# Preparing the first pair of graphs side by side, with early loads of the adjacency and late loads of the weights

## The chip, the cores and the metric

The kernel runs on one core of a Trainium2 chip. The metric is the device time of one execution in microseconds (us), of which the median over several runs is taken. The engines are named as in the profile: PE (TensorE), DVE (VectorE), ACT (ScalarE), POOL (GpSimd) and SP (SyncE, which only issues transfers here).

## The reference

There are 16 graphs of 1024 nodes with 64 channels, a symmetric 0/1 adjacency of 1024 x 1024 and a node mask. Two layers follow each other, each as `x = x + layer(relu(layernorm(x)))`. What matters here is the first one:

```python
neigh = (adj_ > 0) & ~eye
rank = jnp.cumsum(ni, axis=-1) - ni
skip = jnp.where(nb > T, (nb + K - 1) // K, 1)            # T, K = 10, 2
rem = neigh & (sk > 1) & (rank % sk == sk - 1) & mask[:, :, None]
rem = rem | jnp.swapaxes(rem, 1, 2)
adj_d = jnp.where(rem, 0.0, adj_)
vals = jnp.where(nd[..., None], x[:, None, :, :], jnp.inf)
s = jnp.sort(vals, axis=2)
...                                                       # quartiles of s, weighted, summed into agg
h = jax.nn.relu((x + agg) @ W1 + b1)
y = h @ W2 + b2
```

So some edges are dropped, symmetrically; then, for each node and channel, the values of the remaining neighbours are sorted, and their three quartiles make the aggregate. The second layer is three graph convolutions with the undropped adjacency, each with a batch norm, and a last linear layer over all three results.

## The kernel before, in words

The graphs are handled in eight pairs, the 64 channels of the two graphs of a pair lying side by side on the 128 partitions. For each pair there are three kinds of work.

`prepare` (L582) makes the pair ready: it normalizes the rows (`room`, L563), stores them (`h_d`, L598), and for each graph calls `prepare_one`. That loads the adjacency in eight tiles of 128 x 1024 fp32 (`a`, 512 KB, L664, two buffers), makes each into fp8 edges on ACT (L671), checks on DVE that it holds only 0 and 1 (`junk_v`, L673), transposes it on PE (L678) and evicts the transposed tile on ACT (`edgeT`, L681). `edgeT` is stored for the second layer (`adjT_d`, L684), and after that store DVE clears its diagonal in place (L686). Sums over chunks and prefix sums follow on PE (`tot` L646, `cs` L716 and L721), an absolute value on ACT and a comparison on DVE (`stays`, L725 and L726: which edges stay), the symmetric combination on PE (`q`, L736 to L747), and its eviction on ACT with the number of live neighbours (L752). Then nodes are ranked by that number (`keys` L763 on PE, eight signs `junk` L770 on ACT), and `place` (L773, DVE) says where each row goes. POOL scatters the rows to `live_d` (L778) and later fetches them back in that order (`lp`, L794, two buffers); PE transposes them again (L809), ACT evicts (`liveT`, L812), and PE and ACT number the slots of each row (`pr` L845, `r` L851), in two sides: the first 592 columns within `prepare`, the other 432 later through `st.number`.

`gather_block` takes a range of nodes: DVE makes selection matrices (`s`, L987), PE multiplies them with the rows (`pg`, L1018), and ACT copies the result (`g`, L1023). `sort_block` runs a sorting network on DVE over it (L935). There are seven such blocks to a pair, with the sort of one block woven with the gather of the next and with the preparation of the next pair, in parts given by `SHARES`.

The order on each engine comes from the framework's scheduler: it takes what is ready, and among that what was written first in the program. Tiles with one tag share a fixed number of buffers, and a new tile waits until the last reader of an old one is done. In PSUM the preparation has two buffers (`big`), used by the transposes, `tot`, `cs`, `q`, `keys`, `pt` and `pr` of both graphs. `stays`, `junk` and `junk_v` have one buffer; the four fp8 arrays `edge`, `edgeT` and `liveT` of a pair share four (`byte`).

Before all that come constants and the weights: 48 small transfers from ACT's queue (`weight`, `column`, `row`, `both`, L499 to L518) and a few operations on the batch norm's columns (L531 to L537). They are used only by the second layer and the linear parts of the first, in `first_layer` and `next_layer`, which run beside the last pair and after it.

Pair 0 is prepared alone, before the first gather:

```python
ahead = Steps(prepare(0, early))
ahead.rest()
```

Of the kernel before, what the change touches and what calls it, by code (L numbers as in the profile page):

```python
# [10 lines left out]
F32 = mybir.dt.float32  # L11
F16 = mybir.dt.float16
BF16 = mybir.dt.bfloat16
F8 = mybir.dt.float8e4
I32 = mybir.dt.int32
U8 = mybir.dt.uint8
AF = mybir.ActivationFunctionType
ALU = mybir.AluOpType
# [4 lines left out]
P = 128  # L23
C = 64
HID = 128
LN_EPS = 1e-5
BN_EPS = 0.001
# [2 lines left out]

SHARES = (10, 9, 17, 24, 20, 13, 0)
STEPS = 7

MAGIC = 8388608.0

# [362 lines left out]
            pass  # L398


@with_exitstack
def graph_layers_kernel(ctx: ExitStack, tc: tile.TileContext, ins, out: bass.AP):
    nc = tc.nc
    x_d, adj_d, mask_d = ins["x"], ins["adj"], ins["nodemask"]
    NB, N, _ = x_d.shape
    NT = N // P
# [86 lines left out]

    odd = const.tile([P, NB, NT], F32, name="odd")

    def weight(name, rows, cols, twice=False):
        t = const.tile([rows * (1 + twice), cols], F32, name=f"w_{name}")
        for k in range(1 + twice):
            nc.scalar.dma_start(out=t[k * rows : (k + 1) * rows, :], in_=ins[name])  # L499
        return t  # L500

    def column(name, rows, twice=False):
        t = const.tile([rows * (1 + twice), 1], F32, name=f"c_{name}")
        for k in range(1 + twice):
            nc.scalar.dma_start(out=t[k * rows : (k + 1) * rows, :], in_=ins[name].rearrange("(p o) -> p o", o=1))
        return t

    def row(name, cols):
        t = const.tile([P, cols], F32, name=f"r_{name}")
        nc.scalar.dma_start(out=t, in_=ins[name].partition_broadcast(P))  # L510
        return t

    def both(t, src):

        nc.vector.memset(t, 0.0)
        for k in range(2):
            half = slice(k * C, (k + 1) * C)
            nc.scalar.dma_start(out=t[half, half], in_=src)  # L518


    w1 = weight("L0_gnn_W1", C, HID, True)
    w2 = weight("L0_gnn_W2", HID, C)
    b1 = column("L0_gnn_b1", HID)
    b2 = row("L0_gnn_b2", C)
    layers = []
    for i in (1, 2, 3):
        wl = const.tile([P, P], F32, name=f"wl{i}")
        both(wl, ins[f"L1_gnn_W{i}"])
        bl, g, be, m, v = (column(f"L1_gnn_{k}{i}", C, True) for k in ("b", "g", "be", "m", "v"))
        s = const.tile([P, 1], F32, name=f"bn_s{i}")  # L530
        nc.vector.tensor_scalar(s, v, BN_EPS, None, ALU.add)  # L531
        nc.scalar.activation(s, s, AF.Sqrt)
        nc.vector.reciprocal(s, s)
        nc.vector.tensor_tensor(s, s, g, ALU.mult)

        nc.vector.tensor_tensor(m, m, s, ALU.mult)
        nc.vector.tensor_tensor(be, be, m, ALU.subtract)  # L537
        layers.append((wl, bl, s, be))
    wlast = const.tile([P, 3, P], F32, name="wlast")
    for i in range(3):  # L540
        both(wlast[:, i, :], ins["L1_gnn_Wl"][i * C : (i + 1) * C, :])
    blast = row("L1_gnn_bl", C)

    biases = {}

    def bias(value):

        if value not in biases:
            t = const.tile([P, 1], F32, name=f"bias{len(biases)}")
            nc.vector.memset(t, value)  # L550
            biases[value] = t
        return biases[value]

    def rows_of(ap):
        return ap.rearrange("(t p) c -> p t c", p=P)
# [26 lines left out]
        pass  # L582


    def prepare(p, pools):


        work, keep, ps = pools
# [3 lines left out]
        xt, h, sq = room[:, 0], room[:, 1], room[:, 2].rearrange("p x t c -> p (x t) c")  # L592
        for x in range(2):
            nc.sync.dma_start(out=xt[:, x], in_=rows_of(x_d[2 * p + x]))
        flat = "p x t c -> p (x t) c"
        layernorm_relu(work, h.rearrange(flat), xt.rearrange(flat), sq, T2)
        for x in range(2):
            nc.sync.dma_start(out=rows_of(h_d[2 * p + x][:, :]), in_=h[:, x])  # L598
        yield
        st.g = {}  # L600
        st.nvs = keep.tile([P, N], BF16, tag="nvs", bufs=2, name="nvs")
        r0 = keep.tile([P, 2, NT, SPLIT], BF16, tag="r0", name="r0")
        r1 = keep.tile([P, 2, NT, N - SPLIT], BF16, tag="r1", name="r1")
        st.r = (r0, r1)
        find_live, number_slots = [], []
        for x in range(2):
            find_live.append((yield from prepare_one(st, x, pools)))
        for x in range(2):
            number_slots.append((yield from find_live[x]()))
            yield from number_slots[x](0)  # L610


        st.z = keep.tile([P, len(TAUS), N], BF16, tag="z", name="z")
# [15 lines left out]
        yield  # L629
        st.number = itertools.chain(*(number_slots[x](1) for x in range(2)))  # L630
        return st

    def diagonal(e):

# [19 lines left out]
    def prepare_one(st, x, pools):  # L654
# [5 lines left out]
        edge = work.tile([P, NT, N], F8, tag="byte", bufs=4, name="edge")  # L660
        edgeT = work.tile([P, NT, N], F8, tag="byte", bufs=4, name="edgeT")
        def load(t):
            a = work.tile([P, N], F32, tag="a", bufs=2, name="a")
            nc.sync.dma_start(out=a, in_=adj_d[b, t * P : (t + 1) * P, :])  # L664
            return a
# [3 lines left out]
        for t in range(NT):  # L669
            a, coming = coming, load(t + 1) if t + 1 < NT else None  # L670
            nc.scalar.activation(edge[:, t, :], a, AF.Sign, saturate=False)  # L671
            junk = work.tile([P, N], F8, tag="junk_v", name="junk_v")
            nc.vector.scalar_tensor_tensor(  # L673
                junk, a, 1.0, a, ALU.is_equal, ALU.not_equal, accum_out=odd[:, b, t : t + 1], saturate=False
            )
            pt = ps.tile([P, NT, P], F32, tag="big", bufs=2, name="ptE")
            for u in range(NT):
                nc.tensor.matmul(  # L678
                    out=pt[:, u, :], lhsT=edge[:, t, u * P : (u + 1) * P], rhs=ident_h, start=True, stop=True
                )  # L680
            nc.scalar.activation(edgeT[:, :, t * P : (t + 1) * P], pt, AF.Copy, saturate=False)  # L681
            yield

        nc.sync.dma_start(out=adjT_d[b][:, :, :], in_=edgeT)  # L684
# [46 lines left out]
        for t in range(NT):  # L731
            q = ps.tile([P, N], F32, tag="big", bufs=2, name="q")
            for hf in range(NH):
# [15 lines left out]
                        start=False, stop=(u % 4 == 3),  # L749
                    )  # L750

            nc.scalar.activation(  # L752
                edge[:, t, :], q, AF.Relu, bias=bias(-2.0), accum_out=nv[:, t : t + 1], saturate=False
            )
            yield

        key = work.tile([P, NT], F32, tag="key", name="key")
# [30 lines left out]
        def find_live():  # L788
# [16 lines left out]
            for t in range(NT):  # L805
                lp, coming = coming, fetch(t + 1) if t + 1 < NT else None
                pt = ps.tile([P, NT, P], F32, tag="big", bufs=2, name="pt")
                for u in range(NT):
                    nc.tensor.matmul(  # L809
                        out=pt[:, u, :], lhsT=lp[:, u * P : (u + 1) * P], rhs=ident_h, start=True, stop=True  # L810
                    )
                nc.scalar.activation(liveT[:, :, t * P : (t + 1) * P], pt, AF.Copy, saturate=False)  # L812
                yield

            half = slice(x * C, (x + 1) * C)
# [22 lines left out]
            def number_slots(side):  # L838

                j0, j1 = ((0, SPLIT), (SPLIT, N))[side]  # L840
                for u in range(NT):
                    pr = ps.tile([P, N], F32, tag="big", bufs=2, name="pr")
                    for a in range(j0, j1, HALF):
                        sl, o = slice(a, min(a + HALF, j1)), slice(a - j0, min(a + HALF, j1) - j0)
                        nc.tensor.matmul(out=pr[:, o], lhsT=upto, rhs=liveT[:, u, sl], start=True, stop=(u == 0))  # L845
                        if u:
# [1 line left out]
                                out=pr[:, o], lhsT=before[:, u : u + 1].to_broadcast([P, P]), rhs=sums[:, sl],  # L848
                                start=False, stop=True,
                            )  # L850
                    nc.scalar.copy(st.r[side][:, x, u, :], pr[:, : j1 - j0])  # L851
                    if u % 2:
                        yield

# [565 lines left out]
    with ExitStack() as stack:  # L1420
# [7 lines left out]
        with ExitStack() as inner:  # L1428
# [1 line left out]
                inner.enter_context(tc.tile_pool(name="early", bufs=1)), keep,  # L1430
                inner.enter_context(tc.tile_pool(name="ps_early", bufs=1, space=PSUM)),
            )
            ahead = Steps(prepare(0, early))
            ahead.rest()
            st = ahead.result
            first, *_ = gather_block(st, 0, pools)
# [1 line left out]
            for p in range(NP - 1):  # L1438
# [7 lines left out]
                for n in range(last):  # L1446
# [16 lines left out]
                    else:  # L1463
                        weave(sort_block(st, n, pools), gather_block(st, n + 1, pools), steps)
                st = to_come
            for _ in st.number:
                pass

# [69 lines left out]
```

## Time and profile before

| what | value |
|---|---|
| median of three runs | 3166.65 us (3160.47 to 3176.45) |
| the profiled execution | 3163.56 us, of which the span is 3161.8 us |
| busy in the span | PE 82%, DVE 81%, ACT 54%, POOL 20% |
| first edges on ACT (L671) | 32.53 us |
| `place` of graphs 0 and 1 (L773) | 109.09 and 161.33 us |
| first selection of the main phase (`s`, L987) | 205.80 us |
| start of the later pairs' `z` copies on POOL (L1065), pairs 1 and 2 | 511.42 and 811.48 us |

All positions are counted from the start of the span. In the answers quoted below, a timeline row gives the start, the length, the engine, the line and operation, what is written from what with its shape, how many instructions were merged, and in brackets how long the engine had been idle and what released it. A row of groups gives the count, the busy time and the mean of one in ns, and the idle time before.

### The profile page before, as it was taken

To read this page: it belongs to the slowest core of one execution; us is meant where nothing else is said; L and a number is where in the kernel's file an instruction comes from. 1 tells how busy PE (TensorE), PEld (TensorE's weight loads), DVE (VectorE), ACT (ScalarE), POOL (GpSimd) and SP (SyncE) were. 2 spreads that over 40 slices of the span, in tenths; PEclk is the share of its full clock that TensorE was granted. 3 is DMA by queue.
4 is the path that set the end of the run, shared out by engine and by line. 5 is a ranking of instruction groups with operands and counts; after the bars stand their busy time and mean duration, and the time that the engine had idled before them with its cause. 6 is when DMAs were issued, how large, how long until landed. Compare 5 with 4: busy or idle time off the path is not lost.

```text
span 3161.8 us, 67201 instructions
## 1 busy us (share of the span) xinstructions
PE 2599.2 (82%) x27849; PEld 1697.4 (54%) x27849; DVE 2559.8 (81%) x5895; ACT 1696.2 (54%) x3292; POOL 619.5 (20%) x545
## 2 busy tenths in 40 slices
PE   2678978898888889885798889888986688977778
PEld 1445655565556556653565566456643456644445
DVE  4149889998999799989998999899976979963332
ACT  4764666567557755774367557745853223332221
POOL 5110161022102200330022103300422530311110
PEclk9779999999899999997899999999987799988989
DMA  4131022111211212122111211211113011122211
GB/s 138 46 104 60 3 67 70 56 55 52 66 57 54 64 56 68 46 72 47 42 64 51 66 56 57 67 56 63 48 36 75 9 41 26 49 55 54 54 54 42
DMA packets 221082, 177.45 MB, mean 56 GB/s; under 512 B 189024, under 2 KB 189152, under 8 KB 216672
## 3 DMA queue, kind: packets, MB, share of 16 engines
q1 hardware_dynamic: 141824, 125.88, 13.1%
q0 software_dynamic: 17408, 37.81, 3.9%
q10 hardware_dynamic: 61536, 9.39, 1.7%
q8 instruction: 219, 3.59, 0.5%
q14 instruction: 95, 0.78, 0.1%
HBM read 124.44 MB, written 48.55 MB: 55 GB/s over the span
## 4 chain that ended last, share of the span: by engine, by line
DVE 40%; PE 29%; ACT 12%; DMA 8%; issue 6%; another core or an unknown queue 2%; POOL 2%; ACTq 1%; DVEq 0%; POOLq 0%; SPq 0%
PE pg L1018 11%; DVE t L935 10%; DVE s L987 9%; DVE g L935 8%; PE pg L1200 5%; ACT junk L770 3%; DMA a<-in_adj 3%; DMA lp<-live_d 3%; DVE junk_v L673 2%; PE pr L845 2%; DVE g_tails L935 1%; DVE t_tails L935 1%; PE keys L763 1%; PE pf L1216 1%
## 5 line engine op out<-in xcount | busy, mean ns | idle before, releaser
L1018 PE MATMUL pg<-s,hp 128*64 128x400 bf16 (+11 forms) x16848 | 1366.5, 313 | 172.3 <-DVE s L987 138.1
L1018 PEld LDWEIGHTS <-hp 128*64 128x64 bf16 x16848 | 894.5, 112 | 553.9 <-issue 109.6
L987 DVE TENSOR_SCALAR s<-r 128x3200 bf16<-128x3200 bf16 (+25 forms) x1312 | 623.6, 521 | 103.6 <-PE pg L1018 74.9
L778 POOL DMA_INDIRECT live_d<-edge,place x128 | 261.1, 2040 | 1354.3 <-DVE place L773 1149.9
L1023 ACT COPY g<-pg 128x400 f32<-128x400 f32 (+10 forms) x384 | 169.0, 443 | 399.4 <-PE pg L1018 363.1
L935 DVE TENSOR_TENSOR t<-g 128x600 f32<-128x600 f32 (+9 forms) x524 | 315.5, 626 | 34.0 <-ACT g L1023 33.2
L1200 PE MATMUL pg<-adjT,xw 128*64 128x512 fp8e4 x2304 | 284.5, 398 | 52.8 <-ACT xw L1185 25.7
L935 DVE TENSOR_TENSOR g<-t 128x96 f32<-128x96 f32 (+16 forms) x555 | 283.2, 537 | 1.2
L1243 POOL DMA_INDIRECT agg<-agg_d,place x128 | 171.2, 1338 | 495.2 <-PE pt L1131 258.2
L671 ACT ACTIVATE edge<-a 128x1024 fp8e4<-128x1024 f32 x128 | 135.1, 1058 | 214.4 <-DMA a<-in_adj 213.9
L1200 PEld LDWEIGHTS <-xw 128*64 128x64 bf16 x2304 | 140.1, 114 | 182.4 <-issue 42.0
L868 ACT ACTIVATE coef<-z,bias 128x200 f32<-128x200 bf16 (+6 forms) x480 | 173.9, 405 | 102.3 <-DVE agg L950 66.0
L935 DVE TENSOR_TENSOR t<-t 128x192 f32<-128x192 f32 (+20 forms) x447 | 207.8, 475 | 0.2
L871 ACT ACTIVATE coef<-coef,wcol 128x200 f32<-128x200 f32 (+7 forms) x512 | 189.6, 403 | 9.3 <-issue 7.1
L673 DVE SCALAR_TENSOR_TENSOR junk_v<-a 128x1024 fp8e4<-128x1024 f32 x128 | 155.4, 1214 | 24.4 <-DMA a<-in_adj 24.4
L845 PE MATMUL pr<-liveT,upto 128*128 128x512 fp8e4 (+2 forms) x384 | 127.4, 350 | 53.1 <-ACT r L851 46.9
L770 ACT ACTIVATE junk<-keys,minus 128x1024 fp8e4<-128x1024 f32 x128 | 144.3, 1128 | 38.1 <-PE keys L763 34.3
L851 ACT CAST r<-pr 128x592 bf16<-128x592 f32 (+1 forms) x256 | 142.5, 585 | 41.1 <-PE pr L847 32.1
L794 POOL DMA_DIRECT2D lp<-live_d x128 | 89.4, 699 | 376.9 <-PE pt L809 319.3
L812 ACT ACTIVATE liveT<-pt 128x1024 fp8e4<-128x1024 f32 x128 | 130.3, 1034 | 50.5 <-PE pt L809 47.1
L752 ACT ACTIVATE edge<-q,bias 128x1024 fp8e4<-128x1024 f32 x128 | 141.8, 1108 | 22.6 <-PE q L747 22.6
L725 ACT ACTIVATE stays<-cs,back 128x1024 f16<-128x1024 f32 x128 | 136.7, 1111 | 31.1 <-PE cs L721 15.9
(182 smaller groups left out, 3879.4 us busy)
## 6 DMA issues: line engine op xcount, KB each, us to landing
a<-in_adj SPq DMA_DIRECT2D x128, 512.0 KB
adjT_d<-edgeT SPq DMA_DIRECT2D x16, 1024.0 KB
lp<-live_d POOLq DMA_DIRECT2D x128, 128.0 KB
adjT<-adjT_d SPq DMA_DIRECT2D x16, 1024.0 KB
room<-in_x SPq DMA_DIRECT2D x16, 256.0 KB
h_d<-room SPq DMA_DIRECT2D x16, 256.0 KB
h_again<-h_d SPq DMA_DIRECT2D x16, 256.0 KB
xt<-in_x SPq DMA_DIRECT2D x16, 256.0 KB
```

The source lines that it names most:

```text
L673: nc.vector.scalar_tensor_tensor(junk, a, 1.0, a, ALU.is_equal, ALU.not_equal, accum_out=odd[:, b, t : t + 1], saturate=False)
L770: nc.scalar.activation(junk, keys, AF.Sign, bias=minus[:, t : t + 1], accum_out=above[:, t : t + 1], saturate=False)
L778: sent = nc.gpsimd.indirect_dma_start(out=live_d[b][:, :], out_offset=bass.IndirectOffsetOnAxis(ap=place[:, b, t : t + 1], axis=0), in_=ed ...
L845: nc.tensor.matmul(out=pr[:, o], lhsT=upto, rhs=liveT[:, u, sl], start=True, stop=(u == 0))
L868: nc.scalar.activation(coef[:, i, :], z[:, at], AF.Abs, bias=bias(rank - (slots + 1) // 2 + tau), scale=sign)
L871: nc.scalar.activation(coef[:, i, :], coef[:, i, :], AF.Relu, bias=wcol[:, q : q + 1], scale=-w)
L935: nc.vector.tensor_tensor(view(bufs, o, n1, n2), view(bufs, a, n1, n2), view(bufs, b, n1, n2), ALU.max if op else ALU.min)
L987: nc.vector.tensor_scalar(s[:, k, :, us, w0:], r[:, :, us, at + w0 : at + W], float(LIVE + 1 + k0 + k), None, ALU.is_equal)
L1018: summed = nc.tensor.matmul(out=pg[x * C : (x + 1) * C, ks, w0:], lhsT=st.hp[:, part, x, u, :], rhs=s[:, ks, x, u, w0:], start=(whole and ...
L1023: nc.scalar.copy(g[:, k0 : k0 + n, :], pg)
L1200: nc.tensor.matmul(out=pg[cs, :], lhsT=part[:, u, cs], rhs=adjT[x][:, u, sl], start=(u == 0 and k == 0), stop=(u == NT - 1 and k == len(xw ...
L1243: nc.gpsimd.indirect_dma_start(out=agg[:, t, x, :], out_offset=None, in_=agg_d[b][:, :], in_offset=bass.IndirectOffsetOnAxis(ap=place[:, b ...
```

## The change

For pair 0 alone, the adjacency is loaded in 16 transfers into `homes`: buffers of the tags `g`, `t`, `s` and `agg`, which the main phase uses later, and the two of `a`. The steps of the two graphs are written alternately (`side_by_side`), with graph 1 twelve steps behind. The checks (`check`) of pair 0 are written after all its other steps up to the slot numbers. Of its evictions `edgeT`, `liveT`, `r` and the counting one of `q`, every second (`t % 2`) goes to DVE. The weights' loads and the operations on them are written after the second round of the loop over pairs (`p == WEIGHTS`), from SP's queue, and wait for the last gather matmul of pair 2's first block (`behind`).

```diff
+WEIGHTS = 1
+def side_by_side(one, other):
+    while one.step():
+        other.step()
...
+    behind = None
+    def load_weight(t, src):
+        tc.add_manual_dep(
+            nc.sync.dma_start(out=t, in_=src).ins, behind.ins.name,
+            mybir.DependencyInfo(mybir.DependencyClass.Sync, mybir.DependencyReason.DATA),
+            reason="not among the first loads",
+        )
...
-            nc.scalar.dma_start(out=t[k * rows : (k + 1) * rows, :], in_=ins[name])
+            load_weight(t[k * rows : (k + 1) * rows, :], ins[name])
...
+        def check(b, t, a):
+            junk = work.tile([P, N], F8, tag="junk_v", name="junk_v")
+            nc.vector.scalar_tensor_tensor(
+                junk, a, 1.0, a, ALU.is_equal, ALU.not_equal, accum_out=odd[:, b, t : t + 1], saturate=False
+            )
...
+        for k, home in enumerate(homes):
+            nc.sync.dma_start(out=home, in_=adj_d[2 * p + k // NT, k % NT * P : (k % NT + 1) * P, :])
...
+        if homes:
+            one, other = (Steps(prepare_one(st, x, pools)) for x in range(2))
+            for _ in range(4 + NT):
+                one.step()
+            side_by_side(one, other)
+            find_live = Steps(one.result())
+            side_by_side(find_live, other)
+            other.rest()
+            number_slots.append(find_live.result)
+            find_live = Steps(other.result())
+            side_by_side(Steps(number_slots[0](0)), find_live)
+            find_live.rest()
+            number_slots.append(find_live.result)
+            yield from number_slots[1](0)
+            for k, home in enumerate(homes):
+                check(2 * p + k // NT, k % NT, home)
...
+    def evict(st, t, o, i):
+        if st.homes and t % 2:
+            nc.vector.tensor_scalar(o, i, 1.0, None, ALU.mult, saturate=o.dtype != F8)
+        else:
+            nc.scalar.activation(o, i, AF.Copy, saturate=o.dtype != F8)
...
-            nc.scalar.activation(edgeT[:, :, t * P : (t + 1) * P], pt, AF.Copy, saturate=False)
+            evict(st, t, edgeT[:, :, t * P : (t + 1) * P], pt)
...
+            if st.homes and t % 2:
+                nc.vector.tensor_scalar(
+                    edge[:, t, :], q, 3.0, 0.0, ALU.is_equal, ALU.add, accum_out=nv[:, t : t + 1], saturate=False
+                )
...
+            for pool, tag, bufs, free in (
+                (rows, "g", 2, 2), (rows, "g", 2, 2), (rows, "t", 1, 3), (work, "s", 2, 3), (work, "s", 2, 3),
+                (work, "agg", 1, 1), (early[0], "a", 2, 1), (early[0], "a", 2, 1),
+            ):
+                home = pool.tile([P, free, N], F32, tag=tag, bufs=bufs, name="home")
+                homes += [home[:, k] for k in range(free)]
+            ahead = Steps(prepare(0, early, homes))
...
+                if p != WEIGHTS:
+                    continue
+                behind = st.gathered
+                w1 = weight("L0_gnn_W1", C, HID, True)
...                                        # the other weights and the batch norm's columns, as before
```

## Prediction

> **What bounds the kernel now.** I read the page from its slices downwards. The first lines of its part 2 show the start, one digit per 79 us:
>
> ```profile
> PE   2678978898888889885798889888986688977778
> DVE  4149889998999799989998999899976979963332
> ACT  4764666567557755774367557745853223332221
> ```
>
> From the fourth slice on TensorE and VectorE are mostly busy eight or nine tenths. In the two and a half slices before (205 us) they are not. That is the preparation of pair 0, beside which nothing else can run. So I asked for stretches of 10 us (columns: stretch, length, busy us of PE, PE loads, DVE, ACT, POOL, then clock, DMA share, GB/s):
>
> ```profile
> 20.00:30.00 10.00, 0.00 (x0) 0.00 (x0) 1.08 (x7) 0.41 (x2) 9.48 (x26) 1.00 0.10 10
> ...
> 50.00:60.00 10.00, 1.91 (x16) 1.48 (x15) 3.70 (x6) 4.99 (x5) 0.00 (x0) 1.00 0.76 262
> ...
> 180.00:190.00 10.00, 5.28 (x45) 4.41 (x46) 0.00 (x0) 4.25 (x5) 2.14 (x4) 0.50 0.19 57
> ```
>
> No engine is full in these. Adding the stretches from 30 to 210 us gives ScalarE 129 us, VectorE 49 us: ScalarE carries the work while VectorE is nearly free. What they wait for is in the timeline, first ScalarE's:
>
> ```profile
> 31.57 1.06 ACT L563 ACTIVATE room<-room 128x1024 f32<-128x1024 f32 x1 [1.74 <-DMA wlast<-in_L_gnn_Wl]
> 32.53 1.99 ACT L671 ACTIVATE edge<-a 128x1024 fp8e4<-128x1024 f32 x2
> ```
>
> ScalarE's queue issues the weight loads until 31.5 us, so the first adjacency tile, landed at 9.65 us, is not turned into edges before 32.53. VectorE's timeline gives the other marks:
>
> ```profile
> 114.72 1.26 DVE L686 TENSOR_TENSOR edgeT<-edgeT,other_h 128x1024 fp8e4<-128x1024 fp8e4 x1 [5.45 <-DMA adjT_d<-edgeT]
> ...
> 161.33 0.17 DVE L773 TENSOR_SCALAR place<-above 128x8 int32<-128x8 f32 x1 [12.62 <-ACT junk L770]
> ...
> 205.80 1.89 DVE L987 TENSOR_SCALAR s<-r 128x3200 bf16<-128x3200 bf16 x2
> ```
>
> Graph 1 has its transposed edges (edgeT) complete only at 110.1 us, 0.9 us after graph 0's `place` at 109.09; its own `place` follows 52.2 us after graph 0's, and the main phase (first `s`) starts at 205.8 us. After that the pairs follow each other at a fixed distance (first `z` copies on POOL at 511.4 and 811.5 us), so a microsecond won before 205.8 should come off the end.
>
> The price list for the ScalarE rows up to 206 us (busy, mean ns | idle before):
>
> ```profile
> L681 ACT ACTIVATE edgeT<-ptE 128x1024 fp8e4<-128x1024 f32 x16 | 16.2, 1020 | 0.7 <-PE ptE L678 0.6
> L812 ACT ACTIVATE liveT<-pt 128x1024 fp8e4<-128x1024 f32 x16 | 16.0, 1023 | 8.3 <-PE pt L809 8.3
> L851 ACT CAST r<-pr 128x592 bf16<-128x592 f32 (+1 forms) x18 | 11.3, 636 | 2.9 <-PE pr L847 2.4 <-issue 0.3
> ```
>
> and VectorE's nearest row with a PSUM source:
>
> ```profile
> L1188 DVE TENSOR_TENSOR rest<-pw,xw 128x512 f32<-128x512 f32 x48 | 32.8, 684 | 36.7 <-ACT xw L1185 27.6 <-issue 8.4
> ```
>
> **What the Trainium skill says.** "VectorE: DVE Perf Modes", section "Why PSUM operands drop a tier": an fp32 operand in PSUM runs at one element per cycle. The trace agrees (512 columns in 684 ns), so an eviction of 1024 columns should cost about what the fp32 row L673 costs, 1.22 us. "DMA: Bandwidth & Descriptors", section "Queues, rings and completion order": descriptors of one issuing queue are consumed in ring order on each DMA engine. So a store issued on SP after a row of loads comes behind them. The trace before, with two loads in flight at most, does not show that case. "TensorE: Matmul & The Clock Gate", section "What's actually happening": after an idle window the array runs at half rate. The trace agrees: clock 0.50 in 180 to 190 us.
>
> **The change, part by part** (times from the start of the span).
>
> *Weights off the start.* 48 small loads leave ScalarE's queue; they took it to 31.5 us. What holds ScalarE next is the layer norm's input: VectorE's subtraction (L562) ends at 7.9, so the square runs at about 8 and the first sign at about 9 to 10 instead of 32.5. ScalarE gains 22.5 us. The one activation table load (1.28 us, before the first square root) moves in front of the square, where ScalarE idles.
>
> *Loads at once.* Before, a tile load waits for one of two buffers. Now 16 loads, 8.4 MB, stand on SP together. The best stretch of 10 us above moved 262 GB/s; 2 us stretches reach 375. At 262 they take 32 us, at 375 22; I take 300, so 28, and all have landed by about 33. ScalarE needs 16 signs (1.055) and 8 evictions (1.02), 25 us from 9 on, so both graphs have edgeT by about 36, graph 1 having waited until 110. But the store of graph 0's edgeT is queued on SP behind graph 1's loads. Issued near 25, it ends near 37, and the diagonal edit (L686) behind it on VectorE, with the sums (TensorE 2 us, ScalarE 1), lets the slot search (`cs`, L716) start at about 42.5 against 65.2. **Gain 23.** The price of that queue is bounded by 0 and 12 us; I take 9, already inside.
>
> *Graph 0 on.* `cs` and `q` took 28.0 us from 65.2 to the first rank (L770, 93.22), with graph 1's signs between. Without these, and with half of `q` on VectorE, 24. The eight ranks alternate with another graph's work on ScalarE (16 us before, from 93.2 to 109.1); so they still do. `place` of graph 0 near 83 instead of 109.1. **Gain 26 so far.**
>
> *Graph 1 beside it.* `stays` has one buffer, so graph 1's `cs` starts only when graph 0's `q` is over (about 64), and `keys` holds one of the two PSUM slots while ranks run. So side by side is really one stage behind: `cs` of graph 1 runs among graph 0's ranks to about 86, `q` 10, `keys` 3.5, ranks 13 (eight of 1.1 and four liveT evictions of 1.02): `place` of graph 1 near 112 against 161.3. **Gain 49.**
>
> *From there on* 44.5 us before (161.3 to 205.8): eight scatters at 1.28 on POOL, fetches of `lp` through two buffers (17 us for eight), then sums and slot numbers. POOL's and TensorE's latencies set this, not evictions; I take no gain (bounds: 3 lost where graph 0's fetches stand on POOL before graph 1's scatters, 4 won). First `s` near 157.
>
> *Evictions on VectorE.* ScalarE loses 8 each of 1.02, 1.31 (with its accumulator read), 1.02 and 0.64, that is 32 us; VectorE gains 24 of about 1.22 and 8 of about 0.75, 35 us. With 49 before, it stays under 90 of some 125 us. The 16 checks (1.22 + 0.08) come later in its queue, and `s`, `g`, `t` and `agg` are free only when their check is done; with 35 us of VectorE idle that costs nothing. Without that cover it would be at most the 21 us of all checks. Eight slot numbers of the second side (432 columns, about 0.6) fall into the main phase: 4.8 us of VectorE, mostly where it waits for the first gather (60% busy from 207 to 230). I charge 2.
>
> *Weights later.* They go to SP behind the last gather matmul of pair 2's block 0, near 780. 48 issues of 0.33 to 0.62 us hold SP for 16 to 30 us; queued behind it are pair 3's adjacency loads, one in 8 us there, whose readers are ScalarE's signs and VectorE's checks. VectorE gets 3.4 us of memsets and small operations, ScalarE three square roots of 0.2. Bounds 0 and 30; I charge 3.
>
> Sum: 49 - 2 - 3 = 44 us off. From the profiled execution (3163.56, span 3161.8) that is 3119.6; the median of the runs stands 3.1 higher, so I say **3121**.
>
> **Rivals.** *A: the loads are the new wait.* At two-buffer pace (about 180 GB/s between 40 and 55 us) 16 tiles take 47 us and the store follows at 55: `cs` at 61, 4 gained there instead of 23. With graph 1 still pulled in, 25 in all: 3140. For it: the store behind the loads. Against: 262 GB/s with 76% of the DMA share used.
>
> *B: overlap better than I grant.* If TensorE stays warm (its clock was 0.50 in four stretches) and the eight ranks of each graph run back to back (9 us instead of 16, twice), 14 to 21 more are gained, some 62: 3102.
>
> *C: nothing arrives.* The main phase may wait for something else, such as pair 1's preparation, and give the gain back: 3163. Against: after 205.8 VectorE and TensorE are simply full.
>
> *D: slower.* The weights at the head of SP wait for pair 2's gather while pair 3's loads, its signs and its checks stand in order behind; VectorE then stops at a check (it did for 24.4 us in all before, on L673). With 48 issues and the wait it could hold for 60 to 70 us; above 44 it turns the sign: 3185. Against: SP has nothing else urgent there, and the wait is on work that VectorE must do anyway.
>
> **How the numbers follow.** My case 0.50, B 0.15, A 0.17, C 0.08, D 0.10. About 0.5% (16 us) is what a measurement of this kernel can tell from no change. My case, A and B lie beyond it on the fast side: faster 0.82, same 0.08, slower 0.10. The range from 3095 (B with its bound of 4) to 3157 (below A, with the full 21 us of checks or most of SP's hold) leaves out C, D and a tail of B.
>
> **What would show it.** Right: ScalarE's first sign near 10 us, edgeT of both graphs by 40, `place` at about 83 and 112, first `s` near 157, the pairs' distance still 300 us. Wrong: first `s` later than 185; a VectorE wait in the third pair on L673 of tens of us; L686 waiting past 45 us. If first `s` comes at 157 but the end does not move, C or D is true.

## The result, and the profile after

| | median of the runs | profiled execution | its span |
|---|---|---|---|
| before (15 runs beside it) | 3167.62 us | 3163.56 us | 3161.8 us |
| after (15 runs) | 3182.69 us | 3177.61 us | 3175.8 us |

After takes **1.0048** of the time before, with a 95% interval of [1.0024, 1.0073]: some 15 us more, where 44 us less were forecast. The slices of 79 us of the profile after:

```profile
PE   4468978899888889885798899888886689887778
DVE  6259989999899899989997999799976979873332
ACT  5454666568557755774477557745753223332221
```

TensorE's first slice rose from 2 to 4 tenths, but its second fell from 6 to 4: work came forward, and then something stopped it. The stretches of 10 us that the prediction showed, now:

```profile
20.00:30.00 10.00, 1.98 (x16) 1.64 (x17) 9.27 (x21) 8.54 (x9) 5.25 (x11) 1.00 0.99 383
50.00:60.00 10.00, 7.07 (x81) 5.19 (x81) 4.40 (x8) 6.26 (x7) 5.85 (x32) 1.00 0.01 2
180.00:190.00 10.00, 6.20 (x51) 4.08 (x49) 4.69 (x5) 2.71 (x3) 2.68 (x5) 0.67 0.21 67
```

The columns are again stretch, length, busy us of PE, PE loads, DVE, ACT and POOL, then clock, DMA share and GB/s. The core's DMA moves 383 GB/s from 20 to 30 us, and the loads are over before 50 us. ScalarE's timeline has the first and the last sign of the two graphs:

```profile
8.04 1.06 ACT L706 ACTIVATE edge<-home 128x1024 fp8e4<-128x1024 f32 x1 [6.00 <-DMA home<-in_adj]
...
32.16 1.06 ACT L706 ACTIVATE edge<-home 128x1024 fp8e4<-128x1024 f32 x1 [0.56 <-DMA home<-in_adj]
```

All 16 tiles are edges by 33.2 us. And VectorE's timeline: the diagonal edit of each graph (now L719), `place` of each (L811), the first `s` (L1025):

```profile
37.39 1.22 DVE L719 TENSOR_TENSOR edgeT<-edgeT,other_h 128x1024 fp8e4<-128x1024 fp8e4 x1
...
78.69 1.23 DVE L719 TENSOR_TENSOR edgeT<-edgeT,other_h 128x1024 fp8e4<-128x1024 fp8e4 x1 [2.10 <-DMA adjT_d<-edgeT]
...
105.12 0.17 DVE L811 TENSOR_SCALAR place<-above 128x8 int32<-128x8 f32 x1 [1.84 <-ACT junk L808]
161.41 0.17 DVE L811 TENSOR_SCALAR place<-above 128x8 int32<-128x8 f32 x1 [0.82 <-ACT junk L808]
...
211.20 3.69 DVE L1025 TENSOR_SCALAR s<-r 128x3200 bf16<-128x3200 bf16 x4
```

Graph 0's slot search (its first `cs`) begins 23 us earlier than before, its `place` only 4 us, graph 1's `place` not at all, and the main phase starts 5.4 us later. Where the lead goes is in TensorE's waits from 20 to 205 us (total, times, longest). After:

```profile
PE pt L847 <- DMA lp<-live_d: 32.6, 6, 18.3
PE tot L679 <- DVE edgeT L719: 21.7, 2, 16.3
PE pr L883 <- ACT junk L808: 9.6, 1, 9.6
```

Before, the first two stood like this:

```profile
PE tot L646 <- DVE edgeT L686: 14.9, 2, 7.9
...
PE pt L809 <- DMA lp<-live_d: 8.7, 4, 3.3
```

And TensorE's timeline after shows how one graph's wait holds the other:

```profile
38.66 1.90 PE L679 MATMUL tot<-edgeT,pick 128*32 128x512 fp8e4 x16 [16.26 <-DVE edgeT L719]
...
57.25 0.38 PE L769 MATMUL q<-stays,ident 128*128 128x512 f16 x1 [0.85 <-ACT edge L790]
...
58.62 0.61 PE L711 MATMUL ptE<-ident_h,edge 128*128 128x128 bf16 x8
60.11 0.38 PE L769 MATMUL q<-stays,ident 128*128 128x512 f16 x1 [0.88 <-DVE edge L786]
...
79.97 1.90 PE L679 MATMUL tot<-edgeT,pick 128*32 128x512 fp8e4 x16 [5.49 <-DVE edgeT L719]
...
83.22 3.60 PE L801 MATMUL keys<-ident,key 128*128 128x128 f32 x16
...
119.90 1.03 PE L847 MATMUL pt<-ident_h,lp 128*128 128x128 bf16 x8 [18.30 <-DMA lp<-live_d]
120.73 0.63 PE L749 MATMUL cs<-before,sums 128*128 128x512 bf16 x1
```

Four places, from the top. (1) TensorE stands idle from 22.4 to 38.66 for graph 0's diagonal while graph 1's edges lie ready to be transposed. (2) Graph 0's `q` and graph 1's transposes (`ptE`) alternate, one `q` in 2.86 us (2.87 on the mean over the first seven evictions; before, it was 1.44), and each `q` starts only when the one before it has been evicted. (3) Graph 0's key is ready at 76.4 but `keys` runs at 83.22, after graph 1's `tot`, which waited for graph 1's diagonal. (4) Graph 1's last `cs` tiles run at 120.73, behind graph 0's `pt`, which waited 18.3 us for rows that POOL still had to scatter and fetch.

The Trainium skill has two sentences on what is seen here. "PSUM — Partial Sum Buffer", section "Engine vs sequencer instructions", says that matmuls start in program order; place 4 agrees, with 18.3 us. "Perfetto Trace Analysis", section "Optimization Strategy", says that a gap which repeats on an engine can mean that there isn't enough PSUM for the next tile; the 0.85 to 0.91 us before each `q` are such gaps, and in experiment 10 below, with more buffers, `q` takes half the time.

**Theory.** The two PSUM buffers of `big` are handed out in the order in which the tiles are written in the program, and TensorE's queue follows that order. Alternating the writing gives each graph, in effect, one buffer, and lets each wait of one graph stop the other. **Rivals:** evictions fall on the wrong engine, since even tiles of both graphs go to ScalarE; VectorE's evictions are what slows; the queue alone couples the graphs, whatever the buffers. A slower clock is none: from 30 to 210 us TensorE's was 0.77 here and 0.80 before, and 0.78 and 0.77 in experiments 1 and 2, which start the main phase some 23 us sooner than before. A second theory concerns the later pair: the weights there cost more than the 3 us charged.

### The profile page after: what moved, and what is told of

Same layout as the page of the kernel before. It is cut to its first block, busy times and chain, and to the rows that moved or that the text cites. A ratio compares the mean times of both kernels' runs of the same rounds, so it can differ in the third digit from the quotient of the medians.

```text
span 3175.8 us, 67160 instructions
## 1 busy us (share of the span) xinstructions
PE 2596.1 (82%) x27826; PEld 1706.7 (54%) x27849; DVE 2596.7 (82%) x5943; ACT 1664.0 (52%) x3245; POOL 609.2 (19%) x545
## 4 chain that ended last, share of the span: by engine, by line
DVE 43%; PE 26%; ACT 10%; issue 8%; DMA 6%; POOL 4%; another core or an unknown queue 3%; SPq 1%; ACTq 0%; DVEq 0%; POOLq 0%
DVE t L973 11%; PE pg L1056 10%; DVE s L1025 10%; DVE g L973 9%; PE pg L1238 5%; DMA lp<-live_d 3%; DVE junk_v L593 3%; ACT junk L808 2%; DMA a<-in_adj 2%; DVE g_tails L973 1%; PE pr L883 1%; DVE t_tails L973 1%; POOL agg L1281 1%; ACT r L664 1%
## 5 line engine op out<-in xcount | busy, mean ns | idle before, releaser
L1025 DVE TENSOR_SCALAR s<-r 128x3200 bf16<-128x3200 bf16 (+25 forms) x1312 | 624.7, 524 | 100.3 <-PE pg L1056 73.4
L816 POOL DMA_INDIRECT live_d<-edge,place x128 | 249.2, 1947 | 1358.0 <-DVE place L811 1146.2
L706 ACT ACTIVATE edge<-a 128x1024 fp8e4<-128x1024 f32 x112 | 118.3, 1058 | 199.9 <-DMA a<-in_adj 199.3
L664 ACT ACTIVATE liveT<-pt 128x1024 fp8e4<-128x1024 f32 x120 | 122.4, 1035 | 78.8 <-PE pt L847 76.2
L664 ACT ACTIVATE r<-pr 128x592 bf16<-128x592 f32 (+1 forms) x240 | 135.6, 593 | 44.7 <-PE pr L885 35.0
L790 ACT ACTIVATE edge<-q,bias 128x1024 fp8e4<-128x1024 f32 x120 | 132.8, 1108 | 43.5 <-PE q L780 43.4
L1243 DVE TENSOR_SCALAR xT<-xT,bn_s,c_L_gnn_be 128x512 f32<-128x512 f32 x48 | 26.1, 545 | 156.0 <-ACT xT L1242 156.0
```

Of the source, the lines that this page charges most:

```text
L664: nc.scalar.activation(o, i, AF.Copy, saturate=o.dtype != F8)
L816: sent = nc.gpsimd.indirect_dma_start(out=live_d[b][:, :], out_offset=bass.IndirectOffsetOnAxis(ap=place[:, b, t : t + 1], axis=0), in_=ed ...
L1025: nc.vector.tensor_scalar(s[:, k, :, us, w0:], r[:, :, us, at + w0 : at + W], float(LIVE + 1 + k0 + k), None, ALU.is_equal)
```

## The experiments

All times in us from the start of the span; "last ptE" is the start of graph 1's last transpose, "2 to 3" the distance of the `z` copies of pairs 2 and 3 in the profiled execution.

| kernel | last ptE | `place` 0 | `place` 1 | first `s` | 2 to 3 | ratio to before |
|---|---|---|---|---|---|---|
| before | 108.0 | 109.1 | 161.3 | 205.8 | 300.3 | 1 |
| after | 70.1 | 105.1 | 161.4 | 211.2 | 308.3 | 1.0048 [1.0024, 1.0073] |
| 1 weights only | 83.6 | 84.7 | 137.2 | 182.5 | 307.3 | 0.9952 [0.9937, 0.9968] |
| 2 order of before | 80.8 | 80.6 | 133.1 | 183.3 | 308.4 | 0.9958 [0.9941, 0.9975] |
| 3 other parity | 69.2 | 103.4 | 159.8 | 207.7 | 310.0 | 1.0036 [1.0021, 1.0050] |
| 4 all on ScalarE | 66.8 | 103.1 | 159.2 | 205.4 | 307.7 | 1.0032 [1.0015, 1.0050] |
| 5 tiles first | 34.6 | 87.4 | 128.5 | 178.5 | 307.6 | 0.9950 [0.9933, 0.9968] |
| 6 tiles first, ScalarE | 40.7 | 90.3 | 131.7 | 174.6 | 308.0 | 0.9929 [0.9899, 0.9959] |
| 7 own PSUM, order of before | 40.0 | 88.5 | 140.8 | 197.9 | | |
| 9 as 5, weights in the start | 35.4 | 93.9 | 133.7 | 178.4 | 300.5 | 0.9906 [0.9883, 0.9928] |
| 10 own PSUM, alternating | 40.3 | 91.7 | 141.4 | 198.6 | | |
| 11 before, weights on SP in the start | 83.6 | 84.6 | 141.4 | 184.9 | 303.8 | 0.9939 [0.9921, 0.9956] |
| 12 as 9, all on ScalarE | 41.3 | 93.1 | 132.7 | 177.2 | 299.7 | 0.9899 [0.9851, 0.9948] |
| 13 after, weights in the start | 68.9 | 102.5 | 158.9 | 210.5 | 294.3 | 0.9998 [0.9985, 1.0011] |

The numbers are those of the labels, and there is no 8. In 7 and 10 the gather has one PSUM buffer (`pg`) instead of three, to make room; all after the first `s` is slower there (3349 and 3353 us in all), and only the start is read.

**1. The weights alone.** The kernel before, with nothing changed but the weights, which go where the change puts them.

```diff
-            nc.scalar.dma_start(out=t[k * rows : (k + 1) * rows, :], in_=ins[name])
+            load_weight(t[k * rows : (k + 1) * rows, :], ins[name])
...
+                if p != WEIGHTS:
+                    continue
+                behind = st.gathered
```

> The kernel before with one part of the change: the weights' loads go behind pair 2's first gather on SP; no homes, no alternation, no evictions on VectorE. Theory 1 (the alternation of steps took back what the early start won): the first sign on ScalarE falls from 32.5 to about 10 us, two load buffers still pace the tiles, so the first selection s starts about 20 us earlier than 205.8 (near 186) and the whole takes about 0.6% less. Rival (the late weights cost as much in the third pair as they save at the start): s near 186, but the distance between the second and third pair's z copies grows by 15 us or more and the whole is within 0.3% of before or slower.

First `s` came at 182.5, 23.3 earlier, and graph 0's slot search (`look`) at 41.78, with two buffers for the loads, where after has 42.86 with all loads at once. So ScalarE's queue alone gives the 23 us at the head of the start; the early loads add nothing that shows there. The whole time is 15 us under before, not 23: the distance 2 to 3 is 7 longer.

**2. The order of before.** After without `side_by_side`: the graphs are written one behind the other, all else as changed.

```diff
-            side_by_side(one, other)
...
+        find_live = []
+        for x in range(2):
+            find_live.append((yield from prepare_one(st, x, pools)))
+        for x in range(2):
+            number_slots.append((yield from find_live[x]()))
+            yield from number_slots[x](0)
```

> The changed kernel with the steps of pair 0 written in the order of before (graph 0 whole, graph 1 whole, then the two searches), everything else of the change kept: early loads, half of the evictions on VectorE, late weights. Theory 1 (the alternation itself costs): the steps q of graph 0 return to about 1.4 us a tile from 2.87, place of graph 0 comes by 90 us instead of 105, place of graph 1 by 120 to 130 instead of 161, s near 165 to 175, the whole about 1% less than before. Rival (two PSUM slots, the scatter and the fetch limit any order): s stays between 200 and 212 and the whole within 0.5% of before.

Undoing the alternation alone takes 27.9 us off the first `s` and turns 1.0048 into 0.9958: the alternation is what cost the lead. Of what was expected, `q` at 1.44 us a tile and `place` of graph 0 at 80.6 came. But `place` of graph 1 at 133 and the first `s` at 183 miss it, and it gains nothing over experiment 1. Graph 1's last transpose is still at 80.8, 49 us after its last sign is done: the order of before holds it too. It did so in the kernel before already, where ScalarE's last sign and TensorE's next rows read:

```profile
75.59 1.08 ACT L671 ACTIVATE edge<-a 128x1024 fp8e4<-128x1024 f32 x1
```

```profile
91.16 2.02 PE L763 MATMUL keys<-ident,key 128*128 128x128 f32 x16 [1.65 <-DVE key L758]
93.02 0.61 PE L678 MATMUL ptE<-ident_h,edge 128*128 128x128 bf16 x8
95.39 0.61 PE L678 MATMUL ptE<-ident_h,edge 128*128 128x128 bf16 x8 [1.76 <-ACT edgeT L681]
```

Edges were complete at 76.7; the transposes waited for graph 0's `keys`, written ahead of them, and then took 2.1 us each. Up to 93.02 it was the written order that held graph 1, and neither loads nor ScalarE. After that ScalarE sets the pace: it was busy 9.99 of the 10 us from 100 to 110, with evictions of `edgeT` (1.02 us) and ranks (1.11) in turn.

**3 and 4. Which engine evicts.** After, with the parity of graph 1's tiles turned round, and after with all evictions on ScalarE.

```diff
-        if st.homes and t % 2:
+        if st.homes and (t + x) % 2:      # 3
+        if False:                         # 4
```

> The changed kernel with graph 1's evictions on the other engine than graph 0's in the same round: even tiles of graph 0 and odd tiles of graph 1 on ScalarE, the rest on VectorE. Theory 1a (in the alternation each graph has one PSUM slot, so a round is matmul plus eviction of one q tile, 1.4 + 1.3 us, whatever engine evicts): rounds stay at 2.8 to 2.9 us, s at 208 to 213. Rival 1b (the two evictions of a round queue on one engine): rounds fall to about 2.2, 16 rounds save about 10 us, s near 200.

> The changed kernel with all evictions of pair 0 on ScalarE, as before; alternation, early loads and late weights kept. Theory 1a (one PSUM slot to each graph): rounds stay near 2.9 us, places near 105 and 161, s within 4 us of 211. Rival (evictions on VectorE are what made it slow): s earlier by 10 us or more. Opposite rival (they are what kept it from being slower): rounds of 3.5 us, s at 220 or later.

`place` of both graphs moves by under 2.5 us in either. So neither the parity nor VectorE is the cause. VectorE's evictions cost the first `s` some 5.8 us (211.2 against 205.4), but the whole times of 4 and after don't differ by what the intervals can tell. The 205.4 of 4 lies outside the 4 us round 211 that were expected, and the 207.7 of 3 just below its range.

**5 and 6. Both graphs' tiles first.** All transposes of both graphs are written first, then graph 0 to its ranks and graph 1 to its ranks, then the rest; 6 has all evictions on ScalarE besides.

```diff
+            both_of = [Steps(prepare_one(st, x, pools)) for x in range(2)]
+            for one in both_of:
+                for _ in range(1 + NT):
+                    one.step()
+            for one in both_of:
+                one.rest()
+            for one in both_of:
+                find_live = Steps(one.result())
+                find_live.rest()
```

> The changed kernel with only the written order of pair 0 altered: first the eight edge tiles of graph 0 and of graph 1, then the rest of graph 0, the rest of graph 1, and the two searches one after the other. Early loads, evictions on VectorE and late weights as in the change. Theory 2 (the two PSUM buffers of the preparation are given out in the written order, so what is written decides what may run ahead): edgeT of graph 1 is complete by 45 us, its diagonal edit by 50 instead of 78.7 or (in the order of before) 87.6, its place near 112 instead of 161 or 133, s near 162, the whole about 40 us less than before, 1.2%. Rival (scatter, fetch and ScalarE bound the chain whatever is written): place of graph 1 not before 128, s near 180.

> As the kernel with the tiles first, but all evictions of pair 0 on ScalarE. Theory 2 (the order is what counts, the evictions little): places within 8 us of those of the kernel with the tiles first, and from place of graph 1 to s about 45 us as before, where the evictions on VectorE made it 50; whole within 0.3% of that kernel. Rival (ScalarE is the bound once the order is right): place of graph 1 12 us or more later.

The transposes now end at 34.6, as forecast for the change, and `place` of graph 1 comes 33 us earlier than in after. It is still 16 later than the 112 of the prediction. ScalarE's timeline of experiment 5 shows the greater part of why (4.4 of the 16 are there already at graph 0's `place`, 87.4 where 83 was forecast):

```profile
79.04 1.11 ACT L754 ACTIVATE stays<-cs,back 128x1024 f16<-128x1024 f32 x1 [0.86 <-PE cs L750]
80.06 1.11 ACT L804 ACTIVATE junk<-keys,minus 128x1024 fp8e4<-128x1024 f32 x1
...
82.11 1.11 ACT L754 ACTIVATE stays<-cs,back 128x1024 f16<-128x1024 f32 x1 [0.86 <-PE cs L750]
```

While `keys` holds one PSUM buffer, graph 1's `cs` has the other alone: one tile in 3.07 us. Part of that is TensorE's clock, 0.50 from 80 to 90 us; in after, at 0.96 from 86 to 93, the same tile took 2.24. The whole is 0.9950, no better than 1, since `place` to `s` is 50.0 here against 45.3 in 1, and the long distance 2 to 3 is there. With all evictions on ScalarE (6) that stretch is 42.9, and the first `s` 4 us earlier; this and the places, 2.9 and 3.2 later, are as expected for 6.

**7 and 10. Is it the buffers, or the queue?** Graph 1 of pair 0 gets a PSUM buffer of its own, beside the two that graph 0 then has alone; 7 in the order of before, 10 in the alternating order. (The edit holds for every pair, but only the start is read.)

```diff
-            pt = ps.tile([P, NT, P], F32, tag="big", bufs=2, name="ptE")
+            pt = ps.tile([P, NT, P], F32, tag=f"big{x}", bufs=2 - x, name="ptE")
...                                      # and so for tot, nbp, cs, q, keys, pt, nv_all, by and pr
-            pg = ps.tile([P, n, W], F32, tag="pg", bufs=3, name="pg")
+            pg = ps.tile([P, n, W], F32, tag="pg", bufs=1, name="pg")
```

> The order of before with early loads, late weights and evictions on VectorE, but graph 1's preparation has a PSUM buffer of its own (paid for by one buffer instead of three in the gather, so the main phase is slower and only the marks up to s count). Theory 2 (buffers are given out in the written order): with nothing shared, graph 1's edgeT is complete near 40 us although it is written after all of graph 0; diagonal edit near 45 instead of 87.6. Rival (graph 1 was late because the scheduler ranks its work behind graph 0's, or because loads or VectorE's checks were late): diagonal edit still after 80.

> The changed kernel with its alternating order, but pair 0's graph 1 has a PSUM buffer of its own (graph 0 keeps two; the gather has one buffer instead of two to make room, so everything after the first s is slower and the whole time is no measure). Theory 2 (the two graphs hand the same PSUM buffers to each other in the written order): graph 1's transposes are done by 40 to 45 us instead of 70, a q tile of graph 0 takes 2 us or less instead of 2.87, and graph 0's place comes before 98 instead of at 105. Rival (PE's in-order queue alone couples them, whatever the buffers): the transposes still end near 70, the waits on pt and tot stay at 16 to 18 us, place of graph 0 stays at 103 to 106.

In 7 graph 1's last transpose falls from 80.8 (experiment 2) to 40.0, in 10 from 70.1 to 40.3; up to there nothing but the buffers was changed, and the order that the scheduler makes follows from them. In 10 graph 0's evictions of `q` on ScalarE, which are every second tile, and TensorE's longest wait read:

```profile
56.86 1.11 ACT L790 ACTIVATE edge<-q,bias 128x1024 fp8e4<-128x1024 f32 x1 [0.85 <-PE q L780]
59.74 1.11 ACT L790 ACTIVATE edge<-q,bias 128x1024 fp8e4<-128x1024 f32 x1 [1.68 <-PE q L780]
```

```profile
PE pt L847 <- DMA lp<-live_d: 13.6, 5, 9.0
```

So two `q` tiles take 2.88 us, one 1.44, half of after. The 16.3 us on `tot` are gone, those on `pt` fall from 32.6 to 13.6, and `place` comes 13.4 and 20.0 earlier. The rival, a queue that couples whatever the buffers, is refuted for the transposes and `q`, and the 18.3 us for which graph 1's `cs` stood behind graph 0's `pt` are gone too. The 9.0 us that remain end at 156.18, when graph 0's work is over and graph 1's rows are still fetched.

Two limits. With the edit there are three buffers instead of two, and three that both graphs share were not run; so it is shown that the coupling needs few buffers together with the written order, but not that a buffer must belong to one graph. And one buffer alone is no cure: in 7 graph 1's `q` takes 3.89 us a tile, 1.41 in 2, and its `place` and the first `s` come 7.7 and 14.6 us later than in 2.

**9 and 12. Weights in the start.** 5 with the weights on SP behind graph 1's last transpose and `r` on ScalarE; 12 with all evictions there.

```diff
+            nonlocal behind
+            behind = st.turned           # graph 1's last transpose
+            load_weights()
...
-                if p != WEIGHTS:
-                    continue
-                behind = st.gathered
```

> The kernel with the tiles first, with two edits: slot numbers r stay on ScalarE, and the weights are loaded during pair 0's preparation, on SP after the two stores of edgeT, released by graph 1's last transpose, instead of in the third pair. Theory: the 32 us that the weights hold SP lie where SP is idle (from 45 to about 140 us), so the distance from pair 2's to pair 3's z copies returns from 308 to 300 us; s near 158; the whole 48 us less than before, 1.5%. Rival (the 8 us in the third pair are not the weights'): the distance stays near 308 and the whole is as with the tiles first.

> Graph by graph with both graphs' tiles first, loads at once, weights in the start, and all evictions on ACT. If the evictions on DVE cost about 4 to 5 us at the end of the preparation: first s near 173 to 175 instead of 178.4, distance of pair 2 to 3 at 300 to 301, whole time 0.988 to 0.990 of the kernel before. If they are neutral: 0.9906 as with them on DVE.

Both beat the kernel before by about 1%. The first `s` of 9 is where 5 has it, the distance 2 to 3 is back at 300.5, and the whole time falls from 0.9950 to 0.9906, 14 us. These are not the weights' alone: `place` of graph 1 comes 5.2 later than in 5 and the stretch behind it is 5.3 shorter, as `r` is on ScalarE again. The clean test of the weights is 13. The 158 expected for the first `s` was missed by 20, for experiment 5's reason. In 12 the first `s` is 1.2 earlier than 9, where 3 to 5 were expected; 0.9899 and 0.9906 can't be told apart. Where VectorE's evictions are concerned, nothing is gained by them in any pair of runs (after and 4, 5 and 6, 9 and 12).

**11 and 13. The same edit, on before and on after.** 11 is before with the weights moved to SP in the start; 13 is after with the weights in the start and all else left.

> The kernel before, with one thing changed: the weights' loads stand on SP within the start, behind graph 1's last transpose, instead of at the head of ACT's queue. If freeing ACT's queue in the start is what can be gained and the later pair is what takes it back: first s at 181 to 186 instead of 205.8, distance of pair 2 to 3 at 300 to 301, whole time 0.7% under the kernel before (0.992 to 0.994), so better than the same edit with the weights in the later pair (0.9952). If the later place of the weights costs nothing (my prediction's 3 us), it stays at 0.995.

> The changed kernel with one part undone: the weights' loads stand on SP within the start, behind graph 1's last transpose, not in the later pair. If the later pair takes 8 us for them, as the distance of pair 2 to 3 says: that distance is 300 to 302 instead of 307 to 310, first s stays at 210 to 214, and the whole time falls from 1.0048 to about 1.002 of the kernel before (1.001 to 1.004). If the later weights cost nothing and the longer distance is chance: 1.004 to 1.006. What stays above 1.000 is then the later first s (5 us, 0.17%).

11 came out as expected in the first `s` and the whole time, though its distance of 303.8 misses the 300 to 301 expected; against experiment 1 the gain of 0.0013 lies within the intervals, and its own `place` of graph 1 is 4 later, where the batch norm's operations now stand among graph 1's evictions: before its square root at 114.71 ScalarE stood 2.4 us, waiting for VectorE, which had waited for the column to land. 13 is clear: its interval lies below those of after, 3 and 4, whose start differs little (first `s` 205.4 to 211.2, 210.5 in 13). The late weights cost the change 0.34 to 0.50% (against 4 and against after), 11 to 16 us, more than the 8 expected. And 13 is at before's time although its first `s` is 4.7 later; why these 4.7 us don't show in 22 runs is not settled.

What the later pair pays is in three views of after. SP's timeline, the weights from 837.01, the last of `bn` columns, the end, and pair 3's next adjacency load:

```profile
837.01 1.83 SPq L509 DMA_DIRECT2D w_L_gnn_W<-in_L_gnn_W  x3
...
863.53 1.23 SPq L509 DMA_DIRECT2D c_L_gnn_v<-in_L_gnn_v  x2
864.80 3.97 SPq L509 DMA_DIRECT2D wlast<-in_L_gnn_Wl  x6
868.81 0.59 SPq L509 DMA_DIRECT2D r_L_gnn_bl<-in_L_gnn_bl  x1
869.52 1.50 SPq L699 DMA_DIRECT2D a<-in_adj  x2
```

ScalarE's timeline has the signs round that hold. After it stand VectorE's waits of the pair (807 to 1116 us):

```profile
840.24 1.06 ACT L706 ACTIVATE edge<-a 128x1024 fp8e4<-128x1024 f32 x1 [0.29 <-DMA a<-in_adj]
...
874.77 1.06 ACT L706 ACTIVATE edge<-a 128x1024 fp8e4<-128x1024 f32 x1 [7.02 <-DMA a<-in_adj]
```

```profile
DVE s L1025 <- PE pg L1056: 13.2, 8, 5.8
DVE bn_s L1527 <- DMA c_L_gnn_v<-in_L_gnn_v: 4.8, 3, 2.0
```

SP is held 32.4 us by 48 issues, and two signs are 34.5 us apart, where before had at most 14.5 near there (856.14 to 870.67). VectorE itself stands 4.8 us for three columns of the batch norm and spends 15 operations of 0.15 us on them: 7.1 us, near the 8 by which the distance is longer. The row of `s` on `pg` is not in that count: before has 6.6 us of it and 7.1 more that the profile calls remote. All of VectorE's waits in the stretch are 26.2 us in after, 19.0 in before and 14.0 in 13. In seven profiles with late weights that distance is 307.3 to 310.0, in the five others 294.3 to 303.8. Other distances wander by up to 10 us between profiles (1 to 2: 290.1 after, 300.1 before), so one profile alone would not carry this; seven of seven and the interval of 13 do. How far the early microseconds arrive at the end can be read where the weights are in the start: in 9 and 11 the first `s` is 27.4 and 20.9 us earlier than before, and the whole 30 and 19 us shorter.

## Why the prediction was wrong, step by step

**Weights off the start**: right. First sign at 8.04 (9 to 10 forecast), at the price of a second activation table load that the prediction did not have.

**Loads at once**: the marks were right (all edges by 33.2, graph 0's search from 41.9, forecast 42.5), in part by luck. The checks did not come later in VectorE's queue, as the prediction has it: they ran from 8.19 to 37.46, and the diagonal edit followed them at 37.39 without idle time. In experiment 4, where VectorE evicts nothing, they end at 32.22 and the edit comes when the store has landed:

```profile
33.46 1.23 DVE L719 TENSOR_TENSOR edgeT<-edgeT,other_h 128x1024 fp8e4<-128x1024 fp8e4 x1 [1.23 <-DMA adjT_d<-edgeT]
```

So a store can land sooner than was forecast, and in after the checks and evictions on VectorE stood in the way. The cause of the gain was wrong too: experiment 1 has it with two buffers. And "both graphs have edgeT by about 36" failed: graph 1's last eviction ends at 72.67. I took the 110 us of the kernel before for a lack of loads and of ScalarE; `ptE` at 93.02 behind `keys` says that the transposes first waited for their turn, and only then for ScalarE. That line was in the trace.

**Graph 0 on** is the step that failed first: 83 forecast, 105.1 came. The forecast let graph 0 run as if graph 1 beside it cost nothing but ScalarE's time. Search to key took 34.3 instead of 21.6 (`q` at 2.87 a tile), key to first rank 10.7 instead of 2.4 (`keys` behind graph 1's `tot`), the ranks 18.3 instead of about 16: 12.7, 8.3 and 2, less the 0.6 by which the search began early, make the 22 us missing.

**Graph 1 beside it** failed in the same way: 29 us behind graph 0 were forecast, it came 56.3 behind. TensorE's 18.3 us before `pt` are 18 of the 27, and graph 1's `q` beside graph 0's `pt`, 2.84 us a tile where I allowed 10 us for eight, are 12 to 13 more; the rest of the row was then a little shorter. I had written that `keys` holds one of the two buffers, and drew no conclusion for `cs`, `q` and `ptE`.

**From there on**: 49.8 instead of 44.5, outside the bound of 3. Experiment 4, which differs from after only in the engine that evicts, has 46.2: so 3.6 of the 5.3 are VectorE's evictions, for which the prediction charged 2 in the main phase and nothing here. 5 and 6, with 50.0 and 42.9, say the same. Where the other 1.7 go is not shown.

**Evictions on VectorE**: the durations were right (1.22, 0.77 and 0.61 us), the use was not. ScalarE was not what the start waited for, once the weights were off its queue; some 32 us less work for it bought nothing (from 30 to 210 us it is busy 79.9 us where before it was 128.9).

**Weights later** was mis-sized: 3 charged, 8 in the distance, 4 to 16 between whole times. The hold of SP, 32.4 us, passed the upper bound of 30, and I had counted for VectorE its operations but not its wait on each of their columns.

**Slips in the numbers.** "No engine is full" overlooked POOL, busy 9.48 us of the 10 shown from 20 us on. The distance of the pairs, called fixed, runs from 292.8 to 351.5 us within the profile before. The clock was 0.50 in five stretches of 10 us, not four. And 3119.6 and 3.1 make 3122.7, not 3121. None of these decides the outcome.

Of the rivals, C (nothing arrives) is what happened in the start, though inside the preparation and not after it. D's place was right and its direction too, with a cost of some 8 us, not 60 to 70. A is refuted: the core's DMA moved 383 GB/s while the loads ran. B did not come: TensorE's clock from 30 to 210 us was not higher than before (0.77 against 0.80), and graph 0's ranks took 18.3 us.

So the change's gain was real, 23 us from one of its parts. The step that failed is the overlap of the two graphs, put at no cost: two PSUM buffers and one queue in written order let each graph's waits stop the other, which took all of the gain back and 5 us more (first `s` at 211.2, and 183.3 without the alternation). The late weights, charged 3 and mis-sized, added the loss that is measured.

## What to carry to other kernels

Before two chains are woven, list the buffers and the in-order queue that both pass, and walk through them in written order: here, with two buffers between them, each chain had in effect one, and each wait of one stopped the other. When a stage starts long after its inputs are complete, look at what is written ahead of it on its engine, before blaming the loads. Loads that are moved out of an idle start into a full pipeline were paid here at the engine that waited for them; behind the first urgent work of the start (9, 11, 12 and 13) they cost less.

## What the runs showed of the hardware

While sixteen loads of 512 KB stood in one queue, the core's DMA moved 383 GB/s from 20 to 30 us, with the DMA engines 99% busy. The 48 small weight loads took SP 32.4 us to issue, 0.68 us each on the mean, though 31 of them are single columns. An eviction of 1024 fp32 columns from PSUM took 1.22 us on VectorE and 1.01 to 1.02 on ScalarE, and with the two graphs woven a `q` tile took 2.87 us with both engines evicting and 2.88 with ScalarE alone (experiment 4). Where a sign ran ahead of the first square root, as in after, ScalarE loaded an activation table twice in the start (at 0.76 and 12.86 us); before did once (14.71 us).
